# A graph kernel whose edge tables are scattered by GpSimd: edge keys made between the norms, a small first piece, counts dealt among the masks, relation tables read in turn

## The chip, the cores and the metric

The kernel runs on one core of a Trainium2 chip. The metric is the device time of one execution in microseconds (us); lower is better. The "span" of a profiled execution runs from its first to its last instruction; the execution's own time is a little longer than its span.

## The reference

There are N = 384 nodes with 1024 features, and E = 12672 edges with a source, a destination and two types each. All arithmetic is in float32.

```python
h = relu(layernorm(x))
q, k, v = h @ wq.T + bq, h @ wk.T + bk, h @ wv.T + bv
q2, k2, v2 = q @ wiq.T + biq, k @ wik.T + bik, v @ wiv.T + biv      # 16 heads of 64
mask = full((N, N), -inf); mask[src, dst] = softplus(edge_type_weights)[type5 - 1]   # the last edge wins
x = x + softmax(q2 k2^T / 8 + mask) v2 @ wo.T + bo
h = relu(layernorm(x))
y = relu(h @ w_in + b_in)
for l in range(2):                       # relational graph convolution, 6 relations, 4 bases
    counts[r, dst] = number of edges of relation r into dst
    agg = sum over edges of (y @ W[r])[src] / counts[r, dst]        # W[r] = sum_b comp[r, b] basis[b]
    y = batchnorm(relu(agg + y @ root + bias) + y)
x = x + layernorm(y @ w_out + b_out)
```

## The kernel before, in words

**Layout.** Nodes lie on the 128 partitions in three chunks, or features lie on partitions and nodes in the free dimension ("T" tiles such as `hT`). A matrix product of TensorE (PE) on float32 shows in the profile as two matmul records per instruction, a transpose as one. The instruction order of PE, DVE, POOL and SP is written by hand: each of these queues runs in the order in which the program emits its instructions. ACT is ordered by hand in the first norms and from the second half of the attention on.

**Dense work, in order.** Three layer norms of chunks of x (`row_sums`, `row_spread`, `norm_on_act`, `norm`), with transposes by PE into `hT` (`relu_T`, L153); q and q2 (`project`, L397); k, k2 and v (L379, in a seven-product form whose sums of operands DVE makes at L366 and L373); v2 (L514); attention (L553 to L601); the output projection (L605, L675); the second norm and `w_in` (L379 as ps_x); then two graph layers. In a graph layer four products with the bases are made (ps_g, L827 and L833, for b = 0 to 3, each in three parts c), then a product with `root` (L867), then the products of neighbours (L882) with `At`, the mixed relation tables.

**The edges.** The mask and the relation counts are made in DRAM tables: `mtab`, four tables of N x N cells, and `atab`, two tables of N x 6 x N cells. SP fills them with a constant first (L204 and `clear`, L272). A column is 128 edges; there are 99 columns, dealt to the four mask tables (j) in rounds (r), with PER = 27 rounds. POOL writes one column with one indirect DMA: `put_mask` (L262) stores values, `put_count` (L267) adds to what is there. Both are ordered: a scatter waits until the one before it on the same table has landed. Before a column can be written, `find_cells` must have found which of its edges share a cell with another edge of the column: it loads all the keys of the columns (`keys`, L239, from `keys_d`, which POOL's DMA at L181 writes from `keys_n`, L178 to L180), and DVE compares (L251), once for the mask and once for the count. `PIECES` cuts the rounds into pieces, and a piece is found and put as one. `put_rounds` puts the masks of a piece and deals some counts among them: `r // 14` counts after round r, so one after each of the rounds 14 to 26. The other 86 counts follow after the last mask, with the reading of the four mask tables (L303) after the second of them.

**Where the edges' steps stand.** `edge_steps` is a generator. Dense code calls `fill(1)` after a part of q, q2, k, k2 and v, which emits the next step on all the queues. So the step decides behind which dense DVE work and which weight load of SP an edge instruction stands.

**The reading of the counts.** At the end of the attention SP loads the first table relation by relation into `A` (L646); `add_tables` on POOL adds the second table to it by accumulating DMAs (L335): relations 0, 1, 2, then the sums over the node chunks for relations 0 and 1 (`add_up`, L330 and L331), then relations 3, 4, 5. `share(r)` sums over the partitions with a product with ones on PE (ps_cnt, L340), and DVE takes the reciprocal (L342, L343), and POOL multiplies (L344). `mix` (L324) adds the relation's table into `At`. The shares of relations 0 and 1 stand in PE's order after parts c = 1 and c = 2 of base b = 1 of the first layer:

```python
between = {(0, 1, 1): shares(0), (0, 1, 2): shares(1),
           (0, 2, 0): lambda: (mix(0, 0, At), share(2)), (0, 2, 1): mixes(0, 1, 0, 1), ...
```

Of the kernel before, what the change touches and what calls it, by code (L numbers as in the profile page):

```python
# [10 lines left out]
F32 = mybir.dt.float32  # L11
# [6 lines left out]
P = 128  # L18
N = 384
# [17 lines left out]
MT = 4  # L37
PER = 27
PAD = MT * PER

PIECES = (0, 3, 6, 9, 12, 15, 18, 21, 24, PER)
MCELLS, ACELLS = N * N, N * R * N


# [6 lines left out]
def gnn_kernel(ctx: ExitStack, tc: tile.TileContext, out, x, edges, chunks, cols, rows, small,  # L51
# [53 lines left out]
    x_sb = keep.tile([P, NT, D], F32, name="x_sb")  # L105
    for t in range(NT):
        nc.sync.dma_start(x_sb[:, t, :], x[t * P:(t + 1) * P, :])
    cols_sb = const.tile([P, NCOL], F32, name="cols_sb")
    nc.scalar.dma_start(cols_sb, cols)
    small_sb = const.tile([P, 52], F32, name="small_sb")  # L110
# [7 lines left out]
    nc.gpsimd.memset(ones, 1.0)  # L118

    hT = keep.tile([P, KD, N], F32, tag="hT", name="hT")  # L120
    mask8 = keep.tile([P, NT, N], F32, tag="mask8", name="mask8")

    def row_sums(src, n=2):
# [37 lines left out]
    atab = [tables.tile([ACELLS + P, 1], F32, name=f"atab{i}") for i in range(2)]  # L161
    keys_d = tables.tile([PAD, P], I32, name="keys_d")

    def edge_steps(ep):
        nat = ep.tile([EC, 3, P], I32, name="nat")
        nc.sync.dma_start(nat, chunks)
        edges_i = ep.tile([P, 4, EC], I32, name="edges_i")
        nc.sync.dma_start(edges_i, edges)
        none = ep.tile([P, NT * N], F32, tag="V1", name="none")
        nc.gpsimd.memset(none, 8.0 * NEG)  # L170
        zero = ep.tile([P, NT * N], F32, tag="V2", name="zero")
        nc.gpsimd.memset(zero, 0.0)

        yield


        cell_n = ep.tile([EC, P], F32, name="cell_n")
        nc.vector.scalar_tensor_tensor(cell_n, nat[:, 0, :], float(N), nat[:, 1, :], ALU.mult, ALU.add)  # L178
        keys_n = ep.tile([EC, P], I32, name="keys_n")
        nc.vector.scalar_tensor_tensor(keys_n, cell_n, 8.0, nat[:, 2, :], ALU.mult, ALU.add)  # L180
        nc.gpsimd.dma_start(keys_d[:EC], keys_n)  # L181

        own = ep.tile([P, 2, PAD], F32, name="own")
        sr = ep.tile([P, EC], F32, name="sr")
# [14 lines left out]
        nc.vector.tensor_scalar(later, jp, 0.0, None, ALU.is_gt)  # L199
        weigh = ep.tile([P, P], F32, name="weigh")  # L200
        nc.vector.tensor_scalar(weigh, later, 1023.0, 1.0, ALU.mult, ALU.add)
        nc.sync.dma_start(small_sb, small.to_broadcast([P, 52]))
        for i in range(MT):
            nc.sync.dma_start(mtab[i][:MCELLS, :].rearrange("(p f) o -> p (f o)", p=P), none)  # L204


        sp = ep.tile([P, 3, 4], F32, name="sp")
        nc.vector.scalar_tensor_tensor(sp[:, 0, :], small_sb[:, 0:4], -1.0, small_sb[:, 0:4], ALU.mult, ALU.min)
# [24 lines left out]
        def find_cells(p):  # L233

            r0, r1 = PIECES[p:p + 2]
            nt = tables_in(r0)
            keys, cells = [ep.tile([P, MT * 3, P], I32, tag=tag, name=tag, bufs=bufs)[:, :nt * (r1 - r0)]
                           for tag, bufs in (("keys", 3), ("cells", 1))]
            nc.sync.dma_start(keys.rearrange("p (j c) n -> p j (c n)", j=nt),  # L239
                              keys_d.rearrange("(j c) n -> j (c n)", j=MT)[None, :nt, r0 * P:r1 * P]  # L240
                              .to_broadcast([P, nt, (r1 - r0) * P]))
            nc.vector.tensor_scalar(cells, keys, 3, None, ALU.logical_shift_right)

            def rounds(v):
                return v.rearrange("p (j c) -> p j c", j=MT)[:, :nt, r0:r1]

            def find(i, row, mine, times, least):
                for n in range(nt * (r1 - r0)):
                    c = n // (r1 - r0) * PER + r0 + n % (r1 - r0)
                    same = ep.tile([P, P], F32, tag="same", name="same", bufs=2)  # L250
                    nc.vector.scalar_tensor_tensor(same, row[:, n, :], mine[:, c:c + 1], times,  # L251
                                                   ALU.is_equal, ALU.mult, accum_out=count[:, i, c:c + 1])
                off = ep.tile([P, MT, 3], F32, tag="off", name="off", bufs=2)[:, :nt, :]
                nc.vector.scalar_tensor_tensor(off, rounds(count[:, i, :]), least, rounds(away[:, i, :]),
                                               ALU.is_ge, ALU.mult)
                nc.vector.tensor_tensor(rounds(at[:, i, :]), off, rounds(own[:, i, :]), ALU.add)

            find(0, cells, own[:, 0, :], later, 1.0)
            return lambda: find(1, keys, key, weigh, 1024.0)
# [4 lines left out]

        def put_count():
            i, c = next(counts)
            nc.gpsimd.indirect_dma_start(atab[0 if i < 9 else i % 2][:, :],  # L267
                                         bass.IndirectOffsetOnAxis(at[:, 1, c:c + 1], 0),
                                         count[:, 1, c:c + 1], None, compute_op=ALU.add)

# [5 lines left out]
        def put_rounds(p):  # L276

            for r in range(*PIECES[p:p + 2]):
                for j in range(tables_in(r)):
                    put_mask(j * PER + r)  # L280
                for _ in range(r // 14):
                    put_count()

        rest = [find_cells(p) for p in range(3)]
        put_rounds(0)
        put_rounds(1)
        for find_more in rest:
            find_more()
        for step in range(2, 18):
            yield  # L290
            for i in {5: (0,), 6: (1,), 7: (2, 3), 8: (4, 5)}.get(step, (step - 4,) if 10 <= step < 16 else ()):
                clear(i // R, i % R)
            if step in (6, 8, 10, 12, 14, 16):
                find_cells(step // 2)()
            for p in {3: (2,), 9: (3,), 10: (4,), 11: (5,), 16: (6, 7), 17: (8,)}.get(step, ()):
                put_rounds(p)
        yield
        for i in range(EC - 13):
            put_count()
            if i == 1:  # L300
                V = [mask8] + [ep.tile([P, NT, N], F32, tag=f"V{j}", name=f"V{j}") for j in range(1, MT)]
                for v, tab in zip(V, mtab):
                    nc.gpsimd.dma_start(v, tab[:MCELLS, :].rearrange("(t p d) o -> p t (d o)", p=P, t=NT))  # L303
                for v in V[1:]:
                    given = ep.tile([P, NT, N], F32, tag="given", name="given")
                    nc.vector.tensor_scalar(given, v, 4.0 * NEG, None, ALU.is_gt)
                    nc.vector.copy_predicated(mask8, given.bitcast(I32), v)

                for n in range(NT):
                    blk = mask8[:, n, n * P:(n + 1) * P]  # L310
                    bare = ep.tile([P, P], F32, tag="bare", name="bare", bufs=2)
                    nc.vector.scalar_tensor_tensor(bare, blk, 4.0 * NEG, ident, ALU.is_lt, ALU.mult)
                    nc.vector.copy_predicated(blk, bare.bitcast(I32), sp[:, 2, 3:4].to_broadcast([P, P]))
# [14 lines left out]
    def add_up(r):  # L328
        sums[r] = late.tile([P, N], F32, tag="sum", name="sum", bufs=2)
        nc.gpsimd.tensor_tensor(sums[r], A[:, r, 0, :], A[:, r, 1, :], ALU.add)  # L330
        nc.gpsimd.tensor_tensor(sums[r], sums[r], A[:, r, 2, :], ALU.add)  # L331

    def add_tables(tab, *rs):
        for r in rs:
            nc.gpsimd.dma_start(A[:, r], tab[r], accum_op=ALU.add)  # L335

    def share(r):

# [10 lines left out]
    with ExitStack() as inner:  # L349
# [33 lines left out]
            pb, pc, pa = [next_bank(name)[:, :HN] for _ in range(3)]  # L383
            return pa, pb, pc

        def project(w, src, bias, name, on_part=None):

            dst = act_tile(name)
            for part in range(4):
# [4 lines left out]
                for c in cuts:  # L394
                    for o in range(2):
                        for k in range(KD):
                            nc.tensor.matmul(ps[o][:, c], wt_[:, k, o * P:(o + 1) * P], src[:, k, c],  # L397
                                             start=(k == 0 and c.start == 0), stop=(k == KD - 1 and c.stop == N),
                                             skip_group_check=True)
                for o in range(2):  # L400
                    oc = part * 2 + o
                    nc.scalar.activation(dst[:, oc, :], ps[o][:, :N], AF.Identity,
# [11 lines left out]

        boB = ap.tile([P, D], F32, name="boB", bufs=1)
        with tc.tile_pool(name="edge", bufs=1, side="right") as ep:
            xn = ap.tile([P, NT, D], F32, tag="T", name="xn", bufs=4)
            with tc.manual_schedule(engines={mybir.EngineType.Activation}):
                def norm_on_act(t, mv, sd):
# [3 lines left out]
                    nc.scalar.activation(xn[:, t, :], x_sb[:, t, :], AF.Identity, bias=off, scale=sd)  # L423

                half = lambda t: lambda j: x_sb[:, t, j * 512:(j + 1) * 512]
                ms0 = row_spread(row_sums(half(0)))
                st1 = row_sums(half(1))
                norm_on_act(0, *ms0)
                ms1 = row_spread(st1)
                st2 = row_sums(half(2))  # L430
                norm_on_act(1, *ms1)
                ms2 = row_spread(st2)
                relu_T(hT, 0, xn[:, 0, :], (0, 0))
                norm(2, xn[:, 2, :], *ms2, parts=2)
                relu_T(hT, 1, xn[:, 1, :], (1, 0))
                relu_T(hT, 2, xn[:, 2, :], (1, 0))
            steps = edge_steps(ep)
            q = project(wq, hT, BQ, "q")
            T = {}

            def sum_tile(i):
# [180 lines left out]
        for g in range(STEPS + 1):  # L622
# [14 lines left out]
            if f + 2 == STEPS:  # L637
# [4 lines left out]
                tabs = [tab[:ACELLS, :].rearrange("(t p r d) o -> r p t (d o)", p=P, r=R, t=NT) for tab in atab]  # L642
                w_first = [wload(basis[0, 0, part], "w_c") for part in range(3)]
                w_first += [wload(basis[0, 1, part], "w_c") for part in range(2)]
                for r in range(R):
                    nc.sync.dma_start(A[:, r], tabs[0][r])  # L646
                add_tables(tabs[1], 0, 1, 2)
                add_up(0)
                add_up(1)
                add_tables(tabs[1], 3, 4, 5)  # L650
        soft_stack.close()
        xtp = ctx.enter_context(tc.tile_pool(name="xtp", bufs=2, side="right"))

# [350 lines left out]
```

## Time and profile before

| | us |
|---|---|
| three runs, not profiled | 749.03, 751.29 (median), 754.7 |
| the profiled execution, its own time | 755.27 |
| its span | 753.5 |
| PE busy in it | 719.0 (95%) |
| DVE, POOL, ACT busy in it | 431.6, 319.9, 142.3 |

A page of the profile gives busy times of engines, a chain of work that ended last, groups of instructions by source line, and the DMAs. PE's busy time is modelled from matmuls that overlap, so 95% doesn't say that PE is at its peak. Other answers of the trace used here are timelines (start, duration, engine, line, operation, output<-inputs, and in brackets the idle time before it and what ended it), waits by engine, and tables of busy time by stretches of the span. "SPq" and "POOLq" are the sequencers that issue DMAs.

### The profile page before, as it was taken

The numbers are of one execution on the slowest core, as the hardware profiler recorded it, in microseconds if no ns is written. First come the engines' busy times: TensorE is split into PE (matmuls) and PEld (weight loads), VectorE is DVE, ScalarE is ACT, GpSimd is POOL, SyncE is SP. The second block draws the span as 40 slices with busy tenths as digits, with TensorE's granted clock in tenths as the row PEclk, the third lists the DMA queues.
The fourth block names the chain that finished last, engine by engine and source line by source line (L and its number), as shares of the span: only waits on it lengthen the run. The fifth ranks groups of instructions, "written<-read, shape, count | busy, mean of one in ns | idle before, by whom it ended". The sixth has DMA issues, their size and how long they took to land.

```text
span 753.5 us, 7704 instructions
## 1 busy us (share of the span) xinstructions
PE 719.0 (95%) x2776; PEld 465.8 (62%) x2776; DVE 431.6 (57%) x1156; ACT 142.3 (19%) x324; POOL 319.9 (42%) x238
## 2 busy tenths in 40 slices
PE   5999999999999999998999599999999999999996
PEld 5755599999954444445975255555555555555543
DVE  6796428879305699245442379990187676000655
ACT  4111111111102487300211031100013111000200
POOL 1265655678786788576885264410000000120000
PEclk9999999999999999999999799999999999999998
DMA  8877666653455322626225983321003212800001
GB/s 337 321 253 246 186 187 213 196 154 101 124 139 166 57 2 16 195 1 152 17 1 150 258 220 126 120 64 68 0 0 124 77 73 104 293 0 1 0 28 57
DMA packets 41028, 90.94 MB, mean 121 GB/s; under 512 B 19628, under 2 KB 28688, under 8 KB 36766
## 3 DMA queue, kind: packets, MB, share of 16 engines
q1 hardware_dynamic: 19550, 81.98, 31.0%
q0 software_dynamic: 20432, 6.06, 9.3%
q10 hardware_dynamic: 1008, 2.41, 1.0%
q8 instruction: 22, 0.36, 0.2%
q14 instruction: 16, 0.13, 0.0%
HBM read 79.27 MB, written 11.16 MB: 120 GB/s over the span
## 4 chain that ended last, share of the span: by engine, by line
PE 86%; DVE 9%; DMA 2%; issue 1%; ACT 1%; POOL 0%; DVEq 0%; ACTq 0%
PE ps_c L882 12%; PE ps_g L833 12%; PE ps_q L397 11%; PE ps_g L827 10%; PE ps_k L379 6%; PE ps_c L867 6%; PE ps_v L514 6%; PE ps_y L605 5%; PE ps_f L926 4%; PE ps_v L379 3%; PE ps_x L379 3%; DVE same L251 2%; PE ps_o L598 2%; PE ps_s L553 2%; PE ps_pT L587 2%; DMA A<-atab 2%
## 5 line engine op out<-in xcount | busy, mean ns | idle before, releaser
L267 POOL DMA_INDIRECT atab<-count,at x99 | 160.2, 1619 | 51.7 <-issue 26.3
L262 POOL DMA_INDIRECT mtab<-m_val,at x99 | 104.1, 1052 | 67.9 <-DMA mtab<-m_val,at 27.7
L882 PE MATMUL ps_c<-At,H 128*128 128x384 f32 x288 | 93.2, 486 | 0.0
L882 PEld LDWEIGHTS ps_c<-At,H 128*128 128x128 f32 x288 | 54.7, 190 | 38.2
L914 POOL TENSOR_TENSOR x_sb<-x_sb,rowsB 128x1024 f32<-128x1024 f32 x3 | 7.0, 2346 | 159.3 <-DMA rowsB<-in_rows 159.3
L324 DVE SCALAR_TENSOR_TENSOR At<-A,small_sb,At 128x1152 f32<-128x1152 f32 x40 | 62.8, 1634 | 0.0
L833 PE MATMUL ps_g<-w_c,XT 128*128 128x384 f32 x144 | 50.1, 503 | 0.0
L827 PE MATMUL ps_g<-T,S 128*128 128x384 f32 x144 | 49.0, 486 | 0.0
L833 PE MATMUL ps_g<-w_c,XN 128*128 128x384 f32 x144 | 47.6, 486 | 0.0
L514 PE MATMUL ps_v<-w_v,v 128*128 128x512 f32 x96 | 41.9, 594 | 0.0
L397 PE MATMUL ps_q<-hT,w_q 128*128 128x384 f32 (+1 forms) x160 | 41.8, 424 | 0.0
L397 PE MATMUL ps_q<-q,w_q 128*128 128x384 f32 x128 | 41.4, 486 | 0.0
L833 PEld LDWEIGHTS ps_g<-w_c,XT 128*128 128x128 f32 x144 | 28.5, 198 | 20.3 <-issue 2.7
L827 PEld LDWEIGHTS ps_g<-T,S 128*128 128x128 f32 x144 | 27.4, 190 | 19.1
L833 PEld LDWEIGHTS ps_g<-w_c,XN 128*128 128x128 f32 x144 | 27.4, 190 | 19.1
L397 PEld LDWEIGHTS ps_q<-hT,w_q 128*128 128x128 f32 x160 | 28.9, 192 | 12.5
L893 DVE TENSOR_TENSOR XN<-u,XN 128x384 f32<-128x384 f32 x6 | 3.4, 558 | 56.3 <-ACT u L892 56.3
L605 PE MATMUL ps_y<-w_o,attT 128*128 128x512 f32 x80 | 35.0, 595 | 0.0
L379 PE MATMUL ps_k<-T,S 128*128 128x192 f32 x192 | 35.0, 326 | 0.0
L397 PEld LDWEIGHTS ps_q<-q,w_q 128*128 128x128 f32 x128 | 24.3, 190 | 17.0
L344 POOL TENSOR_TENSOR A<-A,rn 128x1152 f32<-128x1152 f32 x6 | 20.4, 3401 | 31.9 <-DVE rn L343 31.9
L773 DVE TENSOR_TENSOR T<-w_c 128x768 f32<-128x768 f32 x24 | 25.3, 1056 | 14.1 <-DMA w_c<-in_basis 14.1
(209 smaller groups left out, 1162.6 us busy)
## 6 DMA issues: line engine op xcount, KB each, us to landing
w_c<-in_basis SPq DMA_DIRECT2D x24, 768.0 KB, 5.9
atab<-zero SPq DMA_DIRECT2D x12, 576.0 KB, 9.6
keys<-keys_d SPq DMA_DIRECT2D x6, 768.0 KB, 10.3
w_c<-in_root SPq DMA_DIRECT2D x6, 768.0 KB, 5.4
w_q<-in_wq SPq DMA_DIRECT2D x4, 1024.0 KB, 10.2
w_q<-in_wiq SPq DMA_DIRECT2D x4, 1024.0 KB, 16.4
w_k<-in_wk SPq DMA_DIRECT2D x4, 1024.0 KB, 6.3
w_k<-in_wik SPq DMA_DIRECT2D x4, 1024.0 KB, 6.2
```

The costliest lines, as they stand in the source:

```text
L262: nc.gpsimd.indirect_dma_start(mtab[c // PER][:, :], bass.IndirectOffsetOnAxis(at[:, 0, c:c + 1], 0), m_val[:, c:c + 1], None)
L267: nc.gpsimd.indirect_dma_start(atab[0 if i < 9 else i % 2][:, :], bass.IndirectOffsetOnAxis(at[:, 1, c:c + 1], 0), count[:, 1, c:c + 1], N ...
L324: nc.vector.scalar_tensor_tensor(At[:, b], A[:, r], w, At[:, b], ALU.mult, ALU.add)
L379: nc.tensor.matmul(ps, a[:, k, :], b[:, k, :], start=start and k == 0, stop=(k == 3), skip_group_check=not start)
L397: nc.tensor.matmul(ps[o][:, c], wt_[:, k, o * P:(o + 1) * P], src[:, k, c], start=(k == 0 and c.start == 0), stop=(k == KD - 1 and c.stop ...
L514: nc.tensor.matmul(ps, v[:, k, t * P:(t + 1) * P], w[k // 4][:, k % 4, :], start=(k == 0), stop=(k == KD - 1))
L605: nc.tensor.matmul(ps, attT[:, k, t * P:(t + 1) * P], w_o[half][k // 4][:, k % 4, :], start=(k == 0), stop=(k == KD - 1))
L827: nc.tensor.matmul(ps, x[:, c], y(c), start=start and c == 0, stop=(c == 2), skip_group_check=not start)
L833: nc.tensor.matmul(ps, block(XT, n, i)[:, c], w[c][:, i, o * HC:(o + 1) * HC], start=(first and c == 0), stop=(c == 2 and (i == 1 or ps is ...
L867: nc.tensor.matmul(pr[o], w[k // 2][:, k % 2, o * P:(o + 1) * P], XT[:, k, :], start=(k == 0), stop=False)
L882: nc.tensor.matmul(pr[o], H_[b][:, n, o * P:(o + 1) * P], At[:, b, n, :], start=False, stop=(b == B - 1 and n == NT - 1))
L926: nc.tensor.matmul(p, XT[:, k, t * P:(t + 1) * P], w[k // 2][:, k % 2, c0:c1], start=(k == 0), stop=(k == KC - 1))
```

## The change

- `keys_n` (128 keys of each of 99 columns) is made, and sent to `keys_d`, between the norms of chunks 1 and 2 of x, instead of after the third chunk's transposes; its source `nat` is loaded by SP right behind x, ahead of the first weights. The sums of x's chunks 1 and 2 on DVE move behind the norm of the chunk before.
- `PIECES` gets a first piece of one round (then 2, then 3 as before). Two of the four fills of mask tables now stand ahead of the second weight load of q on SP, and two behind the load of the first keys. `find_cells` of the fourth piece (rounds 6 to 8) is a step of its own (step 3); the later pieces stay at their steps.
- One count is put after each round from round 7 on (`DEALT`), 20 in all; 79 are left for the end. The first 11 counts, instead of the first 9, go to table 0, since table 1 is not filled yet.
- The relations are read in turn: SP loads the first table's relations 0 and 1; POOL adds the second table's relation r and loads the first table's relation r + 2, for r = 0 to 5, with `add_up(0)` and `add_up(1)` between.
- PE makes 22 products of `ones` with `ones` (128 x 128) ahead of the first transposes; their result isn't used. The third chunk's transposes move behind the first 8 matmuls of q.

```diff
-PIECES = (0, 3, 6, 9, 12, 15, 18, 21, 24, PER)
+DEALT = 7
+PIECES = (0, 1, 3, 6, 9, 12, 15, 18, 21, 24, PER)
...
+    nat = const.tile([EC, 3, P], I32, name="nat")
+    nc.sync.dma_start(nat, chunks)
...
+    ps = next_bank("ps_warm")
+    for _ in range(22):
+        nc.tensor.matmul(ps[:, :P], ones, ones, start=True, stop=True)
...
-    def edge_steps(ep):
-        nat = ep.tile([EC, 3, P], I32, name="nat")
-        nc.sync.dma_start(nat, chunks)
+    def edge_steps(ep, none, zero):
         edges_i = ep.tile([P, 4, EC], I32, name="edges_i")
         nc.sync.dma_start(edges_i, edges)
+        nc.sync.dma_start(small_sb, small.to_broadcast([P, 52]))
+        clear_mask(0)
+        clear_mask(1)
         yield
-        nc.vector.scalar_tensor_tensor(cell_n, nat[:, 0, :], float(N), nat[:, 1, :], ALU.mult, ALU.add)
-        nc.vector.scalar_tensor_tensor(keys_n, cell_n, 8.0, nat[:, 2, :], ALU.mult, ALU.add)
-        nc.gpsimd.dma_start(keys_d[:EC], keys_n)
...
-        for i in range(MT):
-            nc.sync.dma_start(mtab[i][:MCELLS, :].rearrange("(p f) o -> p (f o)", p=P), none)
...
-            nc.gpsimd.indirect_dma_start(atab[0 if i < 9 else i % 2][:, :],
+            nc.gpsimd.indirect_dma_start(atab[0 if i < 18 - DEALT else i % 2][:, :],
...
-                for _ in range(r // 14):
+                if r >= DEALT:
                     put_count()
-        rest = [find_cells(p) for p in range(3)]
-        put_rounds(0)
-        put_rounds(1)
+        rest = [find_cells(0)]
+        clear_mask(2)
+        clear_mask(3)
+        rest += [find_cells(p) for p in (1, 2)]
+        for p in range(3):
+            put_rounds(p)
...
-            if step in (6, 8, 10, 12, 14, 16):
-                find_cells(step // 2)()
-            for p in {3: (2,), 9: (3,), 10: (4,), 11: (5,), 16: (6, 7), 17: (8,)}.get(step, ()):
+            if step in (3, 6, 8, 10, 12, 14, 16):
+                find_cells(max(3, step // 2 + 1))()
+            for p in {8: (3,), 9: (4,), 10: (5,), 11: (6,), 16: (7, 8), 17: (9,)}.get(step, ()):
                 put_rounds(p)
         yield
-        for i in range(EC - 13):
+        for i in range(EC - PER + DEALT):
             put_count()
...
-                ms0 = row_spread(row_sums(half(0)))
-                st1 = row_sums(half(1))
-                norm_on_act(0, *ms0)
-                ms1 = row_spread(st1)
+                norm_on_act(0, *row_spread(row_sums(half(0))))
+                ms1 = row_spread(row_sums(half(1)))
+                nc.vector.scalar_tensor_tensor(cell_n, nat[:, 0, :], float(N), nat[:, 1, :], ALU.mult, ALU.add)
+                norm_on_act(1, *ms1)
                 st2 = row_sums(half(2))
-                norm_on_act(1, *ms1)
+                nc.vector.scalar_tensor_tensor(keys_n, cell_n, 8.0, nat[:, 2, :], ALU.mult, ALU.add)
+                nc.gpsimd.dma_start(keys_d[:EC], keys_n)
                 ms2 = row_spread(st2)
                 relu_T(hT, 0, xn[:, 0, :], (0, 0))
                 norm(2, xn[:, 2, :], *ms2, parts=2)
                 relu_T(hT, 1, xn[:, 1, :], (1, 0))
-                relu_T(hT, 2, xn[:, 2, :], (1, 0))
...
+            q = project(wq, hT, BQ, "q", on_start=last_chunk)
...
-                for r in range(R):
-                    nc.sync.dma_start(A[:, r], tabs[0][r])
-                add_tables(tabs[1], 0, 1, 2)
-                add_up(0)
-                add_up(1)
-                add_tables(tabs[1], 3, 4, 5)
+                for r in range(2):
+                    nc.sync.dma_start(A[:, r], tabs[0][r])
+                for r in range(R):
+                    nc.gpsimd.dma_start(A[:, r], tabs[1][r], accum_op=ALU.add)
+                    if r + 2 < R:
+                        nc.gpsimd.dma_start(A[:, r + 2], tabs[0][r + 2])
+                    if 0 < r < 3:
+                        add_up(r - 1)
```

## The prediction

> **What bounds the kernel now.** I read PE's timeline first, for its gaps, since PE is busy 95% of the span. Two gaps are large. One is the first 9.12 us. The other ends at a row that waits for POOL:
>
> ```profile
> 9.12 5.43 PE L153 MATMUL ps_h<-ident,xn 128*128 128x128 f32 x24 [9.12 <-ACT xn L423]
> ...
> 425.28 1.65 PE L340 MATMUL ps_cnt<-sum,ones 128*128 128x384 f32 x2 [8.89 <-POOL sum L331]
> ```
>
> The table of stretches says what the second gap costs besides: PE comes back at a lower granted clock.
>
> ```profile
> 407.00:426.00 19.00, 10.11 (x31) 5.70 (x30) 4.87 (x6) 0.48 (x1) 5.94 (x5) 0.87 1.08 334
> 426.00:434.00 8.00, 8.00 (x18) 4.42 (x17) 5.35 (x8) 1.44 (x3) 4.19 (x5) 0.67 0.76 160
> 434.00:494.00 60.00, 58.00 (x180) 33.92 (x179) 55.88 (x47) 11.30 (x18) 28.34 (x15) 1.00 0.48 148
> ```
>
> The columns are length, PE, PE's weight loads, DVE, ACT, POOL, clock, DMA share, GB/s. From 425.28 to 433.64 PE makes 16 passes of 384 columns. At full clock one takes 0.3224 (24 of them take 7.74 in the chain), so 8.36 us are spent on 5.16: 3.2 lost. The gap and its cold clock are worth 8.9 + 3.2 = 12.1 us.
>
> The chain of waits and POOL's timeline lead back from there:
>
> ```profile
> 410.01 13.08 DMA A<-atab
> 423.17 1.00 POOL sum L330
> 424.24 1.00 POOL sum L331
> ```
>
> ```profile
> 31.05 1.50 POOL L262 DMA_INDIRECT mtab<-m_val,at  x1 [14.99 <-DVE at L256]
> ...
> 95.97 0.97 POOL L262 DMA_INDIRECT mtab<-m_val,at  x1 [3.52 <-DMA mtab<-m_val,at]
> ...
> 216.85 1.58 POOL L267 DMA_INDIRECT atab<-count,at  x1 [0.30 <-issue]
> ...
> 401.62 1.55 POOL L267 DMA_INDIRECT atab<-count,at  x1 [0.30 <-issue]
> ```
>
> POOL works through one queue of scatters from 31.05 to 403.17. SP may load the first table only at 405.13, and PE meets the end of this at 416.4 (end of L833's second part). So in this stage the wait that ends last is POOL's queue plus the reading behind it: 22.1 us from 403.17 to the second sum's end at 425.23.
>
> **The change, part by part.**
>
> *Keys earlier.* Before, `keys_d` is issued at 15.27 and the first keys are there for DVE at 25.97. In the new order of DVE `keys_n` stands behind the third chunk's statistics. x's first chunk lets DVE start at 4.62; I add up its rows (statistics 1.3, aggregate 0.2, sd 0.15, ACT's root 0.2, reciprocal and offset 0.35, the second chunk's the same, third statistics 1.3, two key operations of 0.28): `keys_n` ends near 10.7, 4.5 us earlier. But DVE, in order, still has to do L186 to L222 (14.87 to 21.9, 7.0 us), now behind the third chunk's second evacuation (PE's transposes for it end near 16.4, DVE 17.1): until 24.1. By then the first, smaller keys (a third of the size) have landed. A piece of one round then costs 0.35 + 4 x 0.273 + 0.4 = 1.85 instead of 4.7 us. First scatter near 26.1: 4.9 us earlier. Past what is it moved? SP: the load for the third part of q stands behind two more of its waits, but its part begins at 34.9; the first load of q2 (before at 23.5) now stands behind the fourth keys, which wait for a free buffer (DVE done near 35), and its first product is near 55.7: 20 us of cover. `nat` ahead of the first weights delays these by 0.45 us; they landed near 9 for a product at 14.3.
>
> *Counts among masks.* The masks' phase takes 31.05 to 216.85, 185.8 us. Seven more counts stand in it, at 1.62 + 0.30 = 1.92: +13.4. But POOL waits 16.2 us for landings between rounds 7 and 14 (waits of 0.6 to 3.5 that end in "DMA mtab"); a scatter there takes up to 8.7 us from issue to the release of the next on its table, and four masks and a count last 7.3 instead of 5.4 us. From round 15 on, where a count already stands in each round, the trace has only two landing waits (1.48 and 0.67, at counts). I take 13 of the 16 as absorbed, so the phase keeps its length and ends at 212; the ends are 209 (all absorbed) and 225 (none). Then 79 counts instead of 86: a count of this phase costs (403.17 - 216.85)/86 = 2.17 with its waits, so -15. **POOL's last count ends at 403.2 - 4.9 - 15 = 383**, between 380 and 397.
>
> *Tables in turn.* Before, six loads of SP and a basis part share the DMA engines (share 1.08), and the first addition takes 13 us. The median to landing is:
>
> ```profile
> A<-atab SPq DMA_DIRECT2D x6, 576.0 KB, 7.4
> A<-atab POOLq DMA_DIRECT2D x6, 576.0 KB, 10.8
> ```
>
> Now four plain loads move from SP to POOL's queue, each one more issue of 1.3 us in order there. The Trainium skill speaks against that: "DMA: Bandwidth & Descriptors", section "SWDGE vs HWDGE vs iDMA", sends plain transfers to SP or ACT, since POOL's are made in software and VectorE can hold it up. The same page's fit for POOL's transfers (section "Anatomy of one DMA — SWDGE (gpsimd) path", 2.0 us + bytes/436e3) would make 3.4 us of 576 KB; the row says 10.8. I take the row, as an upper estimate. Then: table closed 1.96 after the last count (403.17 to 405.13), first load 4.9 (to 410.01), addition 10.8, sum 2.1: the first sum is there 19.8 us after the last count, at 403 (by the fit, 12.4 after it, at 395). PE asks at about 416. **12 us of slack: the gap of 8.9 and the cold clock's 3.2 go, -12.1.** Even at 397 PE would wait under 1 us. By the row the rest of POOL's turn (second and third round of loads, each waiting for its landing) ends near 420; the third sum is then at 425, asked for at 435.
>
> What is late next: the third part of basis 1 (DVE waited 14.1 us for it) stands behind two table loads, not six. SP may issue it when PE has left basis 0, near 404; median landing 5.9 makes 410, PE needs it at 416.6. Behind the last additions it could take the 15.5 of before: +3.4 at most. DVE: after the gap it is busy without a break from 441 to 494 and PE waits 2.0 us for it at 490 (L840 behind two mixes). These follow PE's own shares in order, so they shift with PE; I keep the 2.0 (ends: 0 and +4, if POOL's multiplications fall on more of DVE's operations; a mix takes 2.29 beside them and 1.53 alone).
>
> *Start.* 22 products are 44 passes of 128 columns. The transposes before came at 0.213 us each for 5.5 us after PE's first work, and matmuls at the full rate from 14.66. "TensorE: Matmul & The Clock Gate", Part 1, has the clock go up after about 3.4 us; here it took 5.5, and 5.8 after the gap (425.28 to 431.1). By the trace the 22 take 26 x 0.213 + 18 x 0.107 = 7.5 us from 1.3, until 8.8; by the page 6.4. The first chunk is ready near 8.25, so by either PE is warm, and 0.6 us late at most. Then the chain is no longer PE's: DVE normalises the third chunk (11.6 to 12.6) ahead of the second chunk's evacuation (to 13.25), so q starts at 13.25 instead of 14.34. Eight transposes stand inside it (0.86), and the two or three first slow passes (0.23) go: -1.1 + 0.86 - 0.23 = -0.5, between -1.2 and +0.8.
>
> *Hidden.* The fourth piece's `find_cells` at step 3 is work that was in the first step; DVE has no dense work then. Fills of the first count table end by the same weight load as before (77); the first count is asked for near 80. The mask was ready at 234.9 and first used at 238.29: 3.4 us of slack, about 8 now.
>
> *Sum.* 753.5 - 12.1 - 0.5 = 740.9 of span; the profiled execution's time lies 1.8 above its span: 742.7. That execution is 4.0 above the median of the runs. POOL's landing waits differ by chance and go into the gap one for one, so these 4.0 may be part of the very gap (then 742.7 holds for all runs); if they lie elsewhere, it is 738.7. I take **741.5**, nearer to the first.
>
> **Rivals.**
>
> A. *The gap closes* (forecast): 738 to 743.8. Chance 0.70.
>
> B. *Another wait takes part of the gap*: the basis part lands late (3.4), or DVE, which loses 14 idle us, holds PE at L867 by 4 more, or POOL's turn-taking makes PE wait at the third sum. One of these gives 742.7 + 3 to 4: 746. For it: DVE's unbroken 53 us and a DMA share above 1. Against: all three have some us of slack in the sum. Chance 0.15.
>
> C. *More goes*: the 2.0 at L840 too, and the 4.0 elsewhere: 736.5. Chance 0.08.
>
> D. *It does not do what it says*: the landing waits come back among the trailing counts, and the DMA engines are as full: gap kept, only the start's 0.5 gained, 750.8. Against: start and seven counts are not waits. Chance 0.04.
>
> E. *The mask is late* (slower). Seven counts now stand ahead of the reading of the mask. If no wait is absorbed, the phase ends at 225, the mask is 8.5 later, less 3.4 of slack: +5, and still 747. It becomes slower than before when the mask is ready after 238.3 + 12.6 = 251, that is when the interleaved counts, the first eleven all on one table, make the queue wait 8 us more besides. With +20 us: 751.3 + 7 = 758. Against: from round 15 on, counts among masks wait for almost nothing. Chance 0.03.
>
> **How the numbers follow.** About 1% is what a measurement of this kernel tells from no change: 743.8 and 758.8. A holds 0.70, but its upper end touches 743.8, so I give 0.67 of it to faster; with C: 0.75. B, D and the rest of A are within 1%: 0.22. E: 0.03. The range leaves out D, E and the ends of B and C: 736.5 to 746.5.
>
> **What would show it.** PE's wait at L340 falls from 8.9 to under 1, and the clock reads 1.00 there; POOL's last count ends near 383; its first scatter is near 26; waits for "DMA mtab" sum to 11 to 16 instead of 27.7; q's first matmul is near 13.3. The runs should spread less than 5.7 us, since POOL's chance waits no longer reach PE. Wrong would be: a last count after 397, the mask ready after 238, or a new PE wait at L867 or at basis 1's third part.

## The result, and the profile after

The changed kernel takes 745.6 us (median of 8 runs, 744.38 to 747.49) against 753.0 us for the kernel before (8 runs, 749.03 to 754.7): ratio 0.9908, 95% interval 0.9884 to 0.9932. Forecast were 741.5 (736.5 to 746.5). Its profiled execution took 747.49, with a span of 745.7 (before 753.5). Here and below, medians and ranges count all runs, while ratios leave out slow runs, those more than 1.5% above the fastest of their kernel.

PE's timeline first, at the place of the old gap and behind it:

```profile
413.50 4.03 PE L846 MATMUL ps_g<-w_c,XT 128*128 128x384 f32 x12
417.37 0.81 PE L338 MATMUL ps_cnt<-sum,ones 128*128 128x384 f32 x2
418.02 4.03 PE L846 MATMUL ps_g<-w_c,XT 128*128 128x384 f32 x12
421.89 0.81 PE L338 MATMUL ps_cnt<-sum,ones 128*128 128x384 f32 x2
...
453.94 4.14 PE L846 MATMUL ps_g<-w_c,XT 128*128 128x384 f32 x12 [0.93 <-DVE H L861]
...
480.92 3.80 PE L880 MATMUL ps_c<-XT,w_c 128*128 128x384 f32 x6 [2.20 <-DVE H L853]
```

The first ps_cnt (here L338) has no bracket: PE no longer waits for POOL. Later it waits for DVE twice, and the second wait is followed by six passes in 3.80 us; at full clock six passes take 2.10 (L880 at 476.62). The table of the same stretches as before (length, PE, weight loads, DVE, ACT, POOL, clock, DMA share, GB/s):

```profile
407.00:426.00 19.00, 19.00 (x60) 11.21 (x59) 13.90 (x15) 2.39 (x5) 8.22 (x8) 1.00 1.09 313
426.00:434.00 8.00, 8.00 (x26) 4.74 (x25) 4.34 (x5) 0.48 (x1) 7.92 (x5) 1.00 1.02 260
434.00:494.00 60.00, 56.87 (x171) 32.84 (x171) 59.69 (x47) 10.81 (x17) 23.62 (x11) 0.97 0.29 109
```

The clock reads 1.00 where it read 0.87 and 0.67, but 0.97 in the last row, where it read 1.00. In that row DVE is busy for 59.69 of 60 us, and PE, busy for 56.87, stands idle only in those two waits for it. POOL's timeline shows how the slack came:

```profile
27.84 1.23 POOL L261 DMA_INDIRECT mtab<-m_val,at  x1 [16.27 <-DVE at L255]
...
388.99 1.55 POOL L266 DMA_INDIRECT atab<-count,at  x1 [0.30 <-issue]
396.99 1.36 POOL L659 DMA_DIRECT2D A<-atab  x1 [6.45 <-PE ps_g L846]
...
403.26 0.99 POOL L332 TENSOR_TENSOR sum<-A 128x384 f32<-128x384 f32 x1 [2.03 <-DMA A<-atab]
404.33 1.00 POOL L333 TENSOR_TENSOR sum<-sum,A 128x384 f32<-128x384 f32 x1
```

The bracket at L659 names PE; by its time POOL waits there for SP's first load (issued at 392.15; SP's two took 4.8 us in the median). The last count ends at 390.54 (403.17 before), the first sum is there at 405.3 and PE asks at 417.4: 12 us of slack. The start didn't go as forecast:

```profile
1.27 7.56 PE L129 MATMUL ps_warm<-ones 128*128 128x128 f32 x44 [1.27 <-POOL ones L123]
8.67 1.04 PE L162 MATMUL ps_h<-ident,xn 128*128 128x128 f32 x8
10.41 1.09 PE L162 MATMUL ps_h<-ident,xn 128*128 128x128 f32 x8 [0.70 <-ACT xn L427]
12.95 4.52 PE L395 MATMUL ps_q<-hT,w_q 128*128 128x192 f32 x16 [1.44 <-ACT hT L90]
17.30 0.93 PE L162 MATMUL ps_h<-ident,xn 128*128 128x128 f32 x7
```

PE is warm for its transposes (8 in 1.04 us), stands idle for 0.70 and 1.44 us, and q's first 16 passes then take 4.52 us: the granted clock was half from 13.14 to 16.55.

With stages cut at the first matmul of q, of k, of the first basis product (ps_g) and of the first output product (ps_f), the difference of the two spans is:

| stage | before | after | difference |
|---|---|---|---|
| until q | 14.34 | 12.95 | -1.4 |
| q to k | 82.87 | 85.27 | +2.4 |
| k to ps_g | 290.0 | 290.1 | +0.1 |
| ps_g to ps_f (both graph layers) | 327.82 | 318.73 | -9.1 |
| ps_f to the end | 38.47 | 38.63 | +0.2 |

### The profile page after: what moved, and what is told of

Same layout as the page of the kernel before. It is cut to its first block, busy times and chain, and to the rows that moved or that the text cites. A ratio compares the mean times of both kernels' runs of the same rounds, so it can differ in the third digit from the quotient of the medians.

```text
span 745.7 us, 7797 instructions
## 1 busy us (share of the span) xinstructions
PE 724.6 (97%) x2820; PEld 471.6 (63%) x2820; DVE 435.3 (58%) x1161; ACT 141.8 (19%) x324; POOL 321.0 (43%) x242
## 4 chain that ended last, share of the span: by engine, by line
PE 87%; DVE 10%; issue 1%; ACT 1%; DMA 0%; DVEq 0%; ACTq 0%
PE ps_c L895 12%; PE ps_g L846 12%; PE ps_q L395 11%; PE ps_g L840 9%; PE ps_k L377 7%; PE ps_c L880 6%; PE ps_v L525 6%; PE ps_y L616 5%; PE ps_f L939 4%; PE ps_v L377 4%; PE ps_s L564 3%; PE ps_x L377 3%; PE ps_o L609 2%; PE ps_pT L598 2%; DVE same L250 2%; DVE At L326 2%
## 5 line engine op out<-in xcount | busy, mean ns | idle before, releaser
L261 POOL DMA_INDIRECT mtab<-m_val,at x99 | 102.3, 1034 | 58.5 <-issue 23.5
L846 PE MATMUL ps_g<-w_c,XT 128*128 128x384 f32 x144 | 48.0, 487 | 0.9 <-DVE H L861 0.9
L395 PE MATMUL ps_q<-hT,w_q 128*128 128x384 f32 (+1 forms) x160 | 43.4, 436 | 1.4 <-ACT hT L90 1.4
L577 DVE CUSTOM_DVE_ANT_0 s<-ps_s,mask 128x384 f32<-128x384 f32 x48 | 24.5, 548 | 14.3 <-PE ps_s L564 14.3
## 6 DMA issues: line engine op xcount, KB each, us to landing
A<-atab POOLq DMA_DIRECT2D x10, 576.0 KB, 10.2
```

Of the source, the lines that this page charges most:

```text
L261: nc.gpsimd.indirect_dma_start(mtab[c // PER][:, :], bass.IndirectOffsetOnAxis(at[:, 0, c:c + 1], 0), m_val[:, c:c + 1], None)
L846: nc.tensor.matmul(ps, block(XT, n, i)[:, c], w[c][:, i, o * HC:(o + 1) * HC], start=(first and c == 0), stop=(c == 2 and (i == 1 or ps is ...
```

## The experiments

Each stage time is from the kernel's one profiled execution; ratios are to the kernel before, measured beside it. Two chips were used: the counts alone, the third chunk ahead of q, the first repeat and the first run of the best version were on the second, all others on the first. Which chip gave the result above isn't on record. Line numbers are each kernel's own.

**1. Which part closes the gap?** Reading in turn alone, put into the kernel before:

```diff
-                for r in range(R):
+                for r in range(2):
                     nc.sync.dma_start(A[:, r], tabs[0][r])
-                add_tables(tabs[1], 0, 1, 2)
...
+                for r in range(R):
+                    nc.gpsimd.dma_start(A[:, r], tabs[1][r], accum_op=ALU.add)
+                    if r + 2 < R:
+                        nc.gpsimd.dma_start(A[:, r + 2], tabs[0][r + 2])
+                    if 0 < r < 3:
+                        add_up(r - 1)
```

> The kernel before with one part of the change alone: the relation tables are read in turn (SP loads relations 0 and 1 of the first table, POOL adds and loads the rest). Theory 'one gap, two ways to close it': from the end of the last count to the first sum took 22.1 us before and 14.8 in the changed kernel; with the last count still at 403.2 the first sum comes at 418, PE asks at 416.4, so PE's wait falls from 8.9 to about 1.6 without a cold clock, and the time falls by 10 to 11, to about 742.5. Rival 'the shorter queue did it': reading in turn hardly helps while the queue ends late, less than 3 us, about 750.

Measured: 754.14, ratio 1.0039 (1.0021 to 1.0058). PE's timeline still has waits at ps_cnt, now at the first and the third sum:

```profile
419.17 0.91 PE L340 MATMUL ps_cnt<-sum,ones 128*128 128x384 f32 x2 [1.84 <-POOL sum L331]
423.79 0.81 PE L340 MATMUL ps_cnt<-sum,ones 128*128 128x384 f32 x2
441.99 1.23 PE L340 MATMUL ps_cnt<-sum,ones 128*128 128x384 f32 x2 [3.85 <-POOL sum L331]
```

POOL's own timeline tells why the third is late:

```profile
429.89 1.27 POOL L648 DMA_DIRECT2D A<-atab  x1 [4.32 <-DMA A<-atab]
435.36 1.30 POOL L648 DMA_DIRECT2D A<-atab  x1 [4.20 <-DMA A<-atab]
436.16 3.14 POOL L344 TENSOR_TENSOR A<-A,rn 128x1152 f32<-128x1152 f32 x1
438.74 1.51 POOL L330 TENSOR_TENSOR sum<-A 128x384 f32<-128x384 f32 x1
440.33 1.60 POOL L331 TENSOR_TENSOR sum<-sum,A 128x384 f32<-128x384 f32 x1
```

POOL stands in its queue for the landings of the last two rounds, and the multiplication and the third sum stand behind them. This is the mechanism named in rival B, "POOL's turn-taking makes PE wait at the third sum"; it appears when the last count is late (400.4 here). The expectation that reading in turn is enough fell.

Now the changed kernel without it (the same diff, the other way round):

> The changed kernel with the old way of reading the tables (six loads on SP, then three additions, two sums, three additions on POOL). Theory 'one gap, two ways to close it': last count near 390.5, plus the old 22.1, is 412.6, ahead of the 417.5 at which PE asks; no wait at ps_cnt, and the time stays at the changed kernel's 745.6 within 1. Rival 'reading in turn did it': PE waits again, some 5 us and a cold clock, about 752.

Measured: 746.78, ratio 0.9942 (0.9908 to 0.9977), beside the 754.14 of reading in turn alone. Its last count ends at 389.44, and there is no wait at ps_cnt. So the shorter queue closes the gap, and reading in turn is not needed. That queue has two parts. The counts dealt from round 7 on, in the kernel before, without the early keys (the first 11 counts go to table 0, and the masks of rounds 6 to 8 stand at step 8 instead of 3, as in the change):

```diff
-                for _ in range(r // 14):
+                if r >= 7:
                     put_count()
...
-            for p in {3: (2,), 9: (3,), ...
+            for p in {8: (2,), 9: (3,), ...
...
-        for i in range(EC - 13):
+        for i in range(EC - 20):
```

> The kernel before with one part of the change alone: one count after each round from 7 on (20 in all, 79 at the end). Theory 'a shorter queue is all': seven counts fall into time in which POOL waited for landings; the last count ends 9 to 10 us earlier, near 393.5, and with the old reading (22.1 us) the first sums are there at 415.6, as PE asks (416.4); the wait of 8.9 and the cold clock go, 10 to 12 us, about 741 where the kernel before takes 752. Rival 'the masks pay': the landing waits stay, the mask's phase grows by 13, the last count stays near 403 and so does the time.

Measured: 757.02, ratio 0.9985 (0.9946 to 1.0025). Last count at 399.39, not 393.5; PE still waits 5.5 us at ps_cnt:

```profile
418.75 0.91 PE L340 MATMUL ps_cnt<-sum,ones 128*128 128x384 f32 x2 [2.44 <-POOL sum L331]
426.57 0.91 PE L340 MATMUL ps_cnt<-sum,ones 128*128 128x384 f32 x2 [3.04 <-POOL sum L331]
```

This ran on the second chip, on which the whole change gained nothing either (see 4). And the early keys with the small first piece, without the dealt counts (the changed kernel, its new start included, with the old reading and `for _ in range(r // 14): put_count()`):

> The change without the counts dealt from round 7 on and without the reading in turn: early keys and a first piece of one round, with the 13 counts among masks and the order of reading of before. If early keys and dealt counts add up (k1_counts_only ended its last count 3.8 earlier than before, and both together 13.8 earlier), the last count ends near 393 to 398, the sum is ready 22.1 later (415 to 420) against 416 asked: a wait at ps_cnt of 0 to 4, and a time of 746 to 750. Rival, that early keys alone do nothing because POOL's waits for landings take them back: last count at 402 or later, wait of 6 to 9, time 751 or more. Rival, that early keys alone suffice: last count at 390 or earlier, no wait, 745.

Measured: 749.88, ratio 0.9992 (0.9972 to 1.0013). PE's timeline:

```profile
418.56 0.91 PE L342 MATMUL ps_cnt<-sum,ones 128*128 128x384 f32 x2 [2.80 <-POOL sum L333]
419.31 4.14 PE L848 MATMUL ps_g<-w_c,XT 128*128 128x384 f32 x12
425.79 0.91 PE L342 MATMUL ps_cnt<-sum,ones 128*128 128x384 f32 x2 [2.34 <-POOL sum L333]
```

POOL's queue in these kernels, from its timeline (counts behind the last mask, when the first of them starts, when the last ends), beside what PE makes of it:

| | first mask | counts behind | from | to | us each | ps_g to ps_f |
|---|---|---|---|---|---|---|
| before | 31.05 | 87 | 214.92 | 403.17 | 2.16 | 327.82 |
| counts alone (second chip) | 30.68 | 80 | 218.95 | 399.39 | 2.26 | 324.83 |
| early keys alone | 26.07 | 87 | 207.15 | 398.86 | 2.20 | 324.56 |
| both, old reading | 26.19 | 80 | 213.44 | 389.44 | 2.20 | 317.42 |
| the changed kernel | 27.84 | 80 | 214.71 | 390.54 | 2.20 | 318.73 |

In these executions each part alone ends the queue about 4 us earlier, both together 13.7; and each alone leaves the first sum at 418.5 to 418.7, some 2 to 3 us after PE asks. (Reading in turn alone has the queue of before, and it ended at 400.4 there: some 3 us are chance.) For the early keys this is clear: they make no difference that their runs can tell, measured beside the changed kernel's repeat (0.9932, see 4). For the counts it is not. Their 80 trailing counts took 180.4 us, and 179.8 to 183.9 in the three other executions on the second chip; in the seven others that have 80 of them, those of the first chip and the changed kernel's, they took 173.5 to 176.5. At that pace (an estimate) the counts alone would end at 392.5 to 395.4 and have the first sum, 19.3 later, ahead of the 416.3 at which PE asks. The difference of 4 to 7 us is as large as the 5.6 by which both parts exceed their sum. Whether the counts alone close the gap on the first chip was not run.

**2. The start.** Three and six products of constants put into the two idle stretches ahead of q and of the third chunk's transposes:

```diff
+                for _ in range(3):
+                    nc.tensor.matmul(ps_warm[:, :P], ones, ones, start=True, stop=True)
                 relu_T(hT, 1, xn[:, 1, :], (1, 0))
+                for _ in range(6):
+                    nc.tensor.matmul(ps_warm[:, :P], ones, ones, start=True, stop=True)
```

> The changed kernel with 3 and 6 more products of constants on PE, behind the first and the second chunk's transposes, in time in which PE stood idle (0.9 and 1.4 us). Theory 'idle PE, cold clock': matmuls of q ran at half rate from 13.07 to 16.48 because PE had stood idle most of the 3.4 us before; now q's first 16 passes take 2.6 us instead of 4.5, and the time falls by 1.7 to 1.9, to about 743.8. Rival 'q waits for something else' (its first weights, the evacuations): the first 16 passes stay at 4.5, the time at 745.6.

Measured: 749.82, ratio 0.9964 (0.9937 to 0.999). k starts at 96.59, without a half-rate stretch. But it starts at 96.58 in experiment 1's old reading too, which has no such products: in the profile of the changed kernel the half clock at q was a matter of phase, that is, of when the clock's windows begin (last section). The products bring nothing that shows; the 743.8 expected with them were missed. The third chunk's transposes back ahead of q:

```diff
+                relu_T(hT, 2, xn[:, 2, :], (1, 0))
...
-            q = project(wq, hT, BQ, "q", on_start=last_chunk)
+            q = project(wq, hT, BQ, "q")
```

> The changed kernel with the third chunk's transposes back ahead of q's first matmul (22 products of constants kept). Theory 'the gap is free': PE has nothing else to do from 11.5 to 12.95, so the transposes (0.86 us) cost nothing there and 0.86 inside q; q starts near 13.2 at full clock, k starts 0.6 to 0.7 earlier than in a run of the changed kernel without a cold clock (96.6), near 95.9, and 2.3 earlier than in the profile shown (98.2). DVE's edge work, which stands behind that evacuation, starts some 4 us earlier, the first scatter at 24 instead of 27.8. Time 1 to 2 us less than the changed kernel. Rival 'nothing in it': k starts at 96.6 or later, time unchanged.

Measured: 758.05, ratio 1.0031 (1.0001 to 1.0061), on the second chip, where the gain of 1 to 2 us that was expected can't be told. The start is as expected: q at 13.03, k at 95.74, 0.84 before the 96.58 of the changed kernel's order at full clock; the first mask is at 22.94 instead of 26.2, since DVE's evacuation no longer waits for transposes behind q. The best version (see 4) has the same start on the first chip: k at 95.72, first mask at 22.73. And the changed kernel without its 22 products of constants:

> The changed kernel without the 22 products of constants. If they bring what the prediction has them bring, the first transposes come at 0.213 us instead of 0.109 (16 of them: 1.7 us later) and q starts 0.5 to 1.5 later than 12.95, with its first passes slow until about 14.7; k starts at 97 to 98. Rival: q waits for DVE's third normalisation anyway, so q starts at 12.95 and only the first passes are slow: k at 96.6 to 97.5, and the 22 products are worth under 1 us.

```profile
8.15 1.97 PE L159 MATMUL ps_h<-ident,xn 128*128 128x128 f32 x8 [8.15 <-ACT xn L424]
10.40 1.60 PE L159 MATMUL ps_h<-ident,xn 128*128 128x128 f32 x8 [0.29 <-ACT xn L424]
12.94 2.84 PE L392 MATMUL ps_q<-hT,w_q 128*128 128x192 f32 x16 [0.94 <-ACT hT L90]
```

Measured: 747.24, ratio 0.9952 (0.9933 to 0.9972), beside the changed kernel's 0.9932 (0.9903 to 0.9962). The transposes are slower by 1.4 us in sum, all of it inside waits: q starts at 12.94 and k at 96.53, as with the products. The rival holds for the start: there they are worth nothing. But the runs are slower: 745.9 to 749.12 (18 runs) against 744.21 to 747.91 (12), 1.8 us in the median. In the one profile the loss lies behind k: a half-rate stretch from 356.2 lasts 6.8 us instead of the repeat's 3.4, and PE waits 1.80 us for DVE at base 3, where the changed kernel's two profiles have 0.93 and no wait:

```profile
456.08 4.14 PE L843 MATMUL ps_g<-w_c,XT 128*128 128x384 f32 x12 [1.80 <-DVE H L858]
```

Whether this comes of the products is not shown.

**3. DVE behind the gap.** The mixes of relations 1 and 2 into the tables of bases 2 and 3 moved from the products of base 2 and base 3 to the product with `root`. DVE makes them ahead of the evacuations for which PE waits:

```diff
-                   (0, 2, 0): ..., (0, 2, 1): mixes(0, 1, 0, 1), (0, 2, 2): mixes(0, 1, 2, 3),
+                   (0, 2, 0): ..., (0, 2, 1): mixes(0, 1, 0, 1),
...
-                   (0, 3, 0): mixes(0, 2, 0, 1), (0, 3, 1): lambda: (mix(0, 2, At, (2, 3)), share(4)),
+                   (0, 3, 0): mixes(0, 2, 0, 1), (0, 3, 1): shares(4),
...
+                   (0, 4, 2): lambda: (mix(0, 1, At, (2, 3)), mix(0, 2, At, (2, 3))), (0, 4, 3): mixes(0, 3, 2, 3),
...
```

The mixes that stood there before follow one part later each.

> The changed kernel with two pairs of mixes of the first graph layer (relations 1 and 2, bases 2 and 3; about 3 us of DVE each) moved from bases 2 and 3 to the product with root. Theory 'evacuations queue behind mixes': PE's waits of 0.93 us at base 3 and of 2.2 at root, and the 3.4 us of half clock after the second (1.7 lost), go: 4.8 us, to about 740.8. Rival 'DVE is full': the same work comes due later, PE waits at the products of neighbours instead, and the time stays at 745.6 within 1.

Measured: 745.87 (741.45 to 751.17, 6 runs), not the 740.8 expected; ratio 0.9895 (0.9852 to 0.9938), beside 0.9942 for the changed kernel with the old reading. ps_g to ps_f takes 313.47, 5.3 less than in the changed kernel: both waits and the half-clock stretch are gone. (Against the changed kernel's repeat, below, it is 4.0.) The profiled execution lost as much in code that is the same (k to the attention's first product 145.27 instead of 140.1), so its total says less than the stage; the best version below shows the gain in its runs.

**4. The repeat, and the best version.** The changed kernel again, on the second chip:

> The changed kernel again, beside the others of this call. Theory 'phase of the clock': PE is at half rate for stretches of 3.4 us (or a multiple) wherever it stood idle for most of the stretch before, and where these stretches begin differs from execution to execution; so the profile's loss at 13.1 us (1.7 us) and the one at 480.7 (1.7 us) may each be there or not, and the runs spread by a few us about 745.6. Rival 'same place every time': both are there again.

Measured: 758.36 (749.09 to 770.14), ratio 1.0014 (0.9985 to 1.0044), while the kernel before ran there from 748.28 to 769.31. The gain wasn't seen on that chip: the fastest of 22 runs took 749.09, and of 63 runs of the kernel before 748.28. Its profiled execution (763.7) has no wait at ps_cnt either and takes 317.43 from ps_g to ps_f. What takes the gain back there is open. The version with the old reading, the moved mixes and the third chunk first, on that chip:

> What the runs so far point to, together: the changed kernel with the old reading of the tables (its sums were in time without the change, and POOL's multiplications stood less in DVE's way), the two pairs of mixes moved to the product with root (that part took 313.5 instead of 318.7 us from the first ps_g to the first ps_f), and the third chunk's transposes ahead of q. Expected: no wait of PE above 1 us between 390 and 500, ps_g to ps_f in 312 to 314, k near 95.9; 745.6 - 5 - 1.5 = 739. Rival: the waits come back elsewhere (At late for the products of neighbours), 744 or more.

Measured: 753.73 (741.13 to 771.36), ratio 0.9939 (0.9903 to 0.9975), not the 739 expected; k at 95.74, ps_g to ps_f 313.47. Both were then run side by side on the first chip:

> The kernel x2_best once more, against the same before on another chip. My theory (POOL's queue bounds only through the gap; old reading, two mixes moved to the product with root, third chunk's transposes ahead of q each take about 1 to 5 us of PE's waits): span near 738, 10 us below after's stages in sum: q to k 82.7, k to s 140, ps_g to ps_f 313.5; time 740, ratio to before 0.985 or less. Rival (the gains of single stages are given back elsewhere): within 2 us of after in the same call.

> The changed kernel as it is, beside the others. Ratio 0.991 as at first (745.6 against 753.0); k to s 140, ps_g to ps_f 317.4 to 318.7, start of k 96.6 or 98.2 as the half-rate stretch falls.

| | us | range | ratio to before | k at | ps_g to ps_f |
|---|---|---|---|---|---|
| changed kernel | 745.39 | 744.21 to 747.91 | 0.9932 (0.9903 to 0.9962) | 96.55 | 317.43 |
| best version | 741.15 | 739.5 to 741.36 | 0.9871 (0.9834 to 0.9909) | 95.72 | 313.47 |

The 4.8 us between their spans (744.2 and 739.4) are the 0.84 of the start and the 3.96 of the graph layers. The best version's start and its last stretch:

```profile
11.91 1.11 PE L162 MATMUL ps_h<-ident,xn 128*128 128x128 f32 x8 [0.35 <-DVE xn L155]
13.00 5.28 PE L399 MATMUL ps_q<-hT,w_q 128*128 128x192 f32 x31
```

```profile
434.00:494.00 60.00, 60.00 (x188) 35.35 (x187) 53.23 (x43) 10.82 (x17) 19.17 (x8) 1.00 0.25 95
```

31 passes in 5.28 us is full clock, and PE makes 188 passes in the 60 us in which the changed kernel makes 171. The repeat has reading in turn and takes 317.43 from ps_g to ps_f, as the old reading does: the 1.3 us between 318.73 and 317.42 are not due to the reading.

## Why the prediction was right, and by how much it missed

**The total: inside the range, outside rival A.** A, the forecast, gave 738 to 743.8; 745.6 is nearer to B's 746, yet none of the three waits that B names cost more than 0.2 us above the forecast. That the range held owes something to luck, as what follows shows.

**The gap: right for the profiled execution, a bad one.** "The gap of 8.9 and the cold clock's 3.2 go, -12.1": by the chain of what ended last, the product behind the second ps_cnt starts at 422.70 in place of 433.64 (-10.9), while ps_g began 1.1 later: -12.0. But that is against one execution of before, itself 2.3 above its median of 753.0, and no other of before was profiled. Beside the repeat 49 runs of before were timed: in 11 the mean granted clock was 0.990 or less, as in the profiled one, and they took 754.0 in the median; the other 38 took 750.3. This suggests that most runs of before did not pay the full price of the cold clock. From median to median the change gained 7.4 us and, beside the repeat, 5.5. The reason was half right: reading in turn, to which the forecast gave a part of the slack, gains nothing alone and isn't needed. The 12 us of slack came by errors that cancel: the last count came 7.5 us later than forecast, and from there to the first sum it took 14.8 instead of 19.8, since the first addition, sized at 10.8, had landed 6.3 after its issue began; PE asked 1.4 later.

**POOL's queue: 7 us short.** Forecast was the last count at 383; measured 390.5 and 386.6. The waits of masks for landings fell as expected (the forecast was 11 to 16 instead of 27.7):

```profile
POOL mtab L261 <- DMA mtab<-m_val,at: 15.9, 14, 2.7
```

But "the phase keeps its length and ends at 212": it ended at 216.6. By the early keys alone and both (207.15 and 213.44), the seven counts cost 6.3 of their 13.4 us, where the forecast had 0. So the mask was ready at 235.1 and first used at 239.4, 4.3 us of slack and not 8. The first scatter was forecast at 26.1; the changed kernel has 27.84 in its first profile and 26.17 in the repeat on the first chip, by the phase of PE's clock (below). None of it reached PE, because the slack at ps_cnt was 12 us.

**The start: the step that failed.** "-1.1 + 0.86 - 0.23 = -0.5": its 14.34 for before came from an execution in which the clock rose late. Against that one alone the repeat, with k at 96.55 instead of 97.21, gains 0.7. In two kernels with before's start (reads alone, counts alone) it rose earlier, and q starts at 13.37 and 13.12, k at 96.01 and 95.84. The changed kernel without a half-rate stretch has k at 96.55. Against these the change costs 0.5 to 0.7 at the start, not -0.5: the eight transposes inside q (0.86) are not paid for by q's earlier start (0.2 to 0.4). In the profile of after, the half clock at q adds 1.7.

**DVE: the size missed.** "I keep the 2.0" was the right wait, 2.20 in the profile and 2.0 in the repeat. What the forecast didn't count is the clock. In before six passes behind the same wait took 2.20, in the profile of after 3.80:

```profile
490.47 2.20 PE L867 MATMUL ps_c<-XT,w_c 128*128 128x384 f32 x6 [2.00 <-DVE H L840]
```

A half-rate stretch fell upon it (480.8 to 484.2, 1.7 us), and so it did in 8 of the 11 profiled executions that have this wait of 2.0 or 2.2. The new wait of 0.93, at base 3, is inside rival B's price; the repeat doesn't have it. With 1.0 for the start, 0.9, 0.2 and 1.7 here, -12.1 becomes -8.3; the spans differ by -7.8.

The best version has neither the start's cost nor these waits and takes 741.15. That this is near the forecast of 741.5 doesn't confirm it: the forecast kept the 2.0, and before took 750.9 beside it.

**Landing of the basis part: right.** SP issued it at 404.67 (forecast near 404), and DVE waited 0.2 for it. POOL's loads and additions took 10.2 us in the median to landing; the fit in the Trainium skill ("DMA: Bandwidth & Descriptors"), 3.4, was again far below. The runs spread 3.1 and 3.7 us (under 5.7), beside 5.7 and 10.2 of before; on the second chip they spread 21.

## What to carry to other kernels

A queue that ends late gives little back until it ends before the question is asked: the early keys, 4 us earlier, were worth nothing measurable, and 14 us earlier removed the whole wait. Whatever is then on the path was in the trace before (DVE's 56 of 60 us behind the gap), so plan the next relief with the first: moving two mixes gave 4 us more. Look at more than one execution before a term is sized from a start or a restart of PE. And run the parts of a change on the same chip as the whole.

## What the runs showed of the hardware

- **The clock follows windows of 3.41 us.** In the clock records of each of the 14 profiled executions all changes lie a multiple of 3.41 us apart (in that of after at 6.31, 13.14, 16.55, 480.76 and 484.18). Counted over all these windows: 36 at full rate are followed by half rate, and in each PE was idle for 56% or more of the window; 2955 are followed by full rate, all but 6 of them with less than 56% idle, and none with 60%. From half rate the clock rose after windows with at most 17% idle and stayed down after those with 18% or more. Where the windows begin, the phase, differs from execution to execution.
- **The time to full clock depends on phase.** From PE's first matmul to the granted full clock the executions have 2.8 to 6.1 us (2.8, 3.3 and 5.7 with the start of before), where the prediction weighed 3.4 against 5.5 as if one of them held. "TensorE: Matmul & The Clock Gate", Part 1, of the Trainium skill has a window of that length run freely; that fits. Its spread of 500 ns does not: here it is 3.3 us.
- **A wait of 2 us can cost 1.7 more.** It fills 59% of a window, so it costs a half-rate stretch only if it falls into one window. At the start 0.70 and 1.44 us of idling did so in the profile of after (62% of the window to 13.14); in the repeat, 1.16 and 1.44 fell into two windows (48% and 29%) and cost nothing. Of the six profiled executions with that start two have the stretch.
- **PE's clock reaches POOL.** In the profile of after q's slow passes hold back the third chunk's transposes, so DVE waits 5.09 us for them instead of 3.41 in the repeat, and the first mask comes at 27.84 instead of 26.17:

```profile
17.94 0.69 DVE L97 TENSOR_SCALAR hT<-ps_h 128x512 f32<-128x512 f32 x1 [5.09 <-PE ps_h L162]
```

```profile
16.27 0.69 DVE L97 TENSOR_SCALAR hT<-ps_h 128x512 f32<-128x512 f32 x1 [3.41 <-PE ps_h L162]
```
